# Eight of the 782 row gathers moved from GpSimd's queue to SyncE, and the end of a graph layer's kernel put in another order

## The chip, the cores and the metric

The kernel runs on one core of one Trainium2 chip. The metric is the device time of one execution in microseconds (us). Times are told as the median of several runs; the profile is that of one execution.

## What is computed

There are 6250 nodes with 128 features each and 100,000 edges, which come sorted by their destination. Cut to what matters, the reference is:

```
msg_in = concat([x[src], x[dst], edge_attr])        # 100000 x (128 + 128 + 4)
h = silu(msg_in @ mW1 + mb1)
messages = h @ mW2 + mb2
aggregated = segment_sum(messages, dst)             # 6250 x 128
u = silu(concat([x, aggregated]) @ uW1 + ub1)
updated = u @ uW2 + ub2
y = layer_norm(x + updated) * ln_g + ln_b
out = layer_norm(x + y)
```

## The kernel before, in words

**Tables.** The first layer of the message network is linear before its silu, so the kernel first makes two tables in HBM, one row for each node: `tab_a` holds x @ mW1 for the source's part and `tab_b` x @ mW1 + mb1 for the destination's part (loop over seven parts of x, L367 to L404). The sum of a row of each, and of the attributes' part, is what goes into the silu of an edge.

**Groups of edges.** Edges are taken in 98 groups (`NG`) of 1024, a group being 8 tiles (`G`) of 128 edges; the last group has 6 tiles. For a tile, GpSimd issues one indirect DMA that gathers 128 rows of 512 bytes by the source's index (`fetch`, L273 to L294). The first 5 groups (`RAW`) gather rows of x itself, since the table isn't ready yet; all others gather from `tab_a`. That makes 782 gathers, of which 742 read `tab_a`. Each gather's address list is a column of `src_i`.

**One round of the loop over groups** (L675 to L717), for group g, written out by hand in the order of each engine's queue:

- `load(g + 4)` (L580): SyncE loads 96 rows of `tab_b` from a register address (`mv`, L586) and the attributes of a group (`st`, L587). Every fourth group it loads the destinations of four groups (`near`, L320), and every 14th it reads 14 row numbers into registers (`load_bases`, L344).
- `hidden(g)` (L627): VectorE adds the gathered rows to the product in PSUM, `s = ga + pre` (L635); ScalarE takes the silu into `h` (L636).
- `products(g + 2)` (L614): TensorE makes the destination's and the attributes' part of a later group, `pre` (L618).
- `node_matrix(g + 3)` and `edge_matrix(g + 1)` (L591, L604): VectorE makes 0/1 matrices from the destinations.
- `by_nodes(g)` (L652): TensorE sums `h` by destination into a window of 96 nodes, `pt` (L647); a round or two later `add` puts it into `acc` (L660) and every fourth group the edge counts into `deg` (L665).
- `fetch(g + 2, begun[g + 2], summing[g])` from group 14 on (L703): GpSimd's gathers of two groups ahead. The first of the eight waits for the first matmul of `products(g + 2)`, and the fifth for the first matmul of the sums of group g. The rows have six buffers.

**Nodes.** As soon as all edges of four tiles of nodes are summed, a generator `node_batch` (L466) does the second half of the layer for them. Each `advance` takes it one step on: load xs and copy the sums; three matmuls of y (L509 to L511); silu (L514); one matmul that adds ub2 (L516) and n matmuls with uW2 (L525); the residual and the moments (L527); square root; z and its moments (L534 to L543); square root; shift (L547); the output (L555); its DMA from SyncE (L559). There are 12 such batches of up to 4 tiles; a last one of 2 tiles has to wait for the last edges and is called `final`.

**The end** (L719 to L757). The last group's add, silu and sums are cut into `piece(0, n - 2)` and `piece(n - 2, n)`. In the queue of VectorE the batch next to last (`before`, of 3 tiles) has its step L527 ahead of the first piece and its step L534 to L543 between the two pieces. Then `final` runs its steps from the three matmuls of y on.

Of the kernel before, what the change touches and what calls it, by code (L numbers as in the profile page):

```python
# [8 lines left out]
F32 = mybir.dt.float32  # L9
I32 = mybir.dt.int32  # L10
# [14 lines left out]
def kernel(  # L25
# [57 lines left out]
    MADE = 3  # L83
    NQ = 4
    NM = 5
    BT = 4
    NC = 10
    EC = E // NC
# [177 lines left out]
    ea_d = dram.tile([ED, NG * GE], F32, name="ea_d")  # L266
    near_d = dram.tile([NG, GE], U8, name="near_d")
    rows, bases, near = {}, {}, {}

    def tiles_of(g):  # L270
        return min(G, -(-(E - g * GE) // P))

    def fetch(g, *after):  # L273

        rows[g] = gath.tile([P, G, H], F32, name="ga")
        for i in range(tiles_of(g)):
            ins = nc.gpsimd.indirect_dma_start(  # L277
                out=rows[g][:, i, :],
                out_offset=None,
                in_=x if g < RAW else tab_a[:, :],  # L280
                in_offset=bass.IndirectOffsetOnAxis(
                    ap=src_i[:, g, i : i + 1] if g else src_0[:, i : i + 1], axis=0
                ),
            )
            part, at = divmod(i * len(after), G)
            if after and at == 0 and after[part]:
                tc.add_manual_dep(
                    ins.ins,
                    after[part].ins.name,
                    mybir.DependencyInfo(  # L290
                        mybir.DependencyClass.Sync, mybir.DependencyReason.DATA
                    ),
                    reason="TensorE keeps up with the gathers",
                )  # L294
# [72 lines left out]
    for k, (i0, n) in enumerate(parts):  # L367
        if k + 1 < len(parts):
            turn_x(*parts[k + 1])

        tb = x_sb[:, i0 : i0 + n, :]
        ta = tpool.tile([P, G, H], F32, name="t", bufs=2)
        for j0, m in groups(n, G // 2):
            pm = wide().rearrange("p (i s) f -> p i s f", s=2)
            for j in range(m):
                cols = slice((i0 + j0 + j) * P, (i0 + j0 + j + 1) * P)
                ins = nc.tensor.matmul(pm[:, j], xT[:, cols], w1, start=True, stop=True)  # L377
            own = slice(j0, j0 + m)
            nc.scalar.copy(ta[:, own], pm[:, :m, 0, :])
            nc.vector.tensor_add(  # L380
                tb[:, own], pm[:, :m, 1, :], b1[:, None, :].to_broadcast([P, m, H])
            )
        nc.sync.dma_start(by_node(tab_a)[:, i0 : i0 + n, :], ta[:, :n])
        nc.sync.dma_start(by_node(tab_b)[:, i0 : i0 + n, :], tb)
        table.append(ins)
        if k == 0:
            attributes(0)
        if k == 1:
            fetch(2, *table)
            for t in mv:  # L390
                nc.sync.dma_start(t[W:], mW1[2 * H :])
        if k == 2:
            fetch(3, None, table[2])
        if k == 3:
            destination_lists()
            attribute_rows(0)
            turn_rows(0)
        cols = slice(i0 * P, NW if i0 + n == NT else (i0 + n) * P)
        nc.vector.memset(acc[:, cols], 0.0)
        if k == 4:  # L400
            fetch(4, *table[3:])
            destinations(0)
            load_bases(0)
            turn_rows(1)  # L404
# [27 lines left out]
    ub2_row = consts.tile([1, H], F32, name="ub2_row")  # L432
    g_b = consts.tile([P, H], F32, name="g_b")
    b_b = consts.tile([P, H], F32, name="b_b")
    raw_w = {}

    def load_weights():
        for name, shape in (("w2", [P, H]), ("u1a", [P, H]), ("mb2", [P, 1])):
            raw_w[name] = work.tile(shape, F32, name=f"raw_{name}", bufs=1)
        nc.sync.dma_start(raw_w["w2"], mW2)  # L440
        nc.sync.dma_start(raw_w["u1a"], uW1[P:])
        nc.sync.dma_start(raw_w["mb2"], mb2.rearrange("(f o) -> f o", o=1))
        nc.sync.dma_start(u1x, uW1[:P])
        nc.sync.dma_start(u2, uW2)
        nc.sync.dma_start(ub1_col, ub1.rearrange("(f o) -> f o", o=1))
        nc.sync.dma_start(ub2_row, ub2.rearrange("(o f) -> o f", o=1))
        for t, row in ((g_b, ln_g), (b_b, ln_b)):
            nc.sync.dma_start(t, row.rearrange("(o f) -> o f", o=1).to_broadcast([P, H]))

    def fuse_weights():  # L450
# [15 lines left out]
    def node_batch(i0, n, work, new, y, final=False):  # L466
# [9 lines left out]
        def flat(t):  # L476
            return t[:, :n].rearrange("p i f -> p (i f)")
# [27 lines left out]
        if final:  # L505
            xb = new("xb")
            nc.vector.tensor_add(xb[:, :n], xs[:, :n], b_b[:, None, :].to_broadcast([P, n, H]))
        y = y()
        nc.tensor.matmul(flat(y), u1x, xT[:, cols], start=True, stop=False)  # L509
        nc.tensor.matmul(flat(y), w2u, sums, start=False, stop=False)  # L510
        nc.tensor.matmul(flat(y), mb2u, counts, start=False, stop=True)  # L511
        yield
        uT = new("uT")
        nc.scalar.activation(flat(uT), flat(y), AF.Silu, bias=ub1_col)  # L514
        yield
        nc.tensor.matmul(  # L516
            y[:, :n],
            ones[0:1, :],
            ub2_row[:, None, :].to_broadcast([1, n, H]),
            start=True,  # L520
            stop=False,
        )
        by_p = flat(uT).rearrange("k (p j) -> k p j", j=n)
        for i in range(n):
            nc.tensor.matmul(y[:, i, :], by_p[:, :, i], u2, start=False, stop=i == n - 1)  # L525
        yield
        nc.vector.tensor_add(y[:, :n], y[:, :n], xs[:, :n])  # L527
        mv = moments(y)
# [47 lines left out]
    NST = 5  # L576
    nodes = edges.enter_context(tc.tile_pool(name="nodes", bufs=1))
    stbuf = [held.tile([K1, GE], F32, name=f"st{k}") for k in range(NST)]

    def load(g):  # L580

        if g % NQ == 0 and g:
            destinations(g)
        if g % RB == 0 and g:
            load_bases(g)
        nc.sync.dma_start(mv[g % NM][:W], tab_b[bass.ds(bases[g], W), :])  # L586
        nc.sync.dma_start(stbuf[g % NST][W:], ea_d[:, g * GE : (g + 1) * GE])  # L587
# [39 lines left out]
    def hidden(g):  # L627
        h = hbuf[g % NH]
        ga = rows.pop(g)
        n = tiles_of(g)  # L630
        s = pre.pop(g)
        if g >= RAW:
            ps = s
            s = work.tile([P, G, H], F32, name="s")
            nc.vector.tensor_add(s[:, :n], ga[:, :n], ps[:, :n])  # L635
        nc.scalar.activation(h[:, :n], s[:, :n], AF.Silu)  # L636
        return h

# [36 lines left out]
    for g in range(NG):  # L675
# [10 lines left out]
                attribute_rows(c)  # L686
        if g + LEAD < NG:
            load(g + LEAD)
        last = g >= NG - 1
        if not last:  # L690
            h[g] = hidden(g)
# [21 lines left out]
        for i0, n, first in batches[:-1]:  # L713
            if g == (first if first >= NG - 3 else first + 1):
                running.append(node_batch(i0, n, *node_tiles(nodes, node_y)))
        for _ in range(2 if g >= NG - 6 else 1):
            advance(running)  # L717

    g = NG - 1  # L719
# [18 lines left out]
    )  # L738
    while running:
        advance(running)  # L740
    for _ in range(2):
        next(before)
    next(final)

    nc.scalar.activation(primed, ones[0:1, 0:1], AF.Silu)
    add(g - 1, pt.pop(g - 1))
    pt[g] = degrees(g)
    piece(0, n - 2)
    next(before)
    piece(n - 2, n)  # L750
    add(g, pt.pop(g))
    for _ in range(2):
# [161 lines left out]
```

## Time and profile before

| | |
|---|---|
| median of 3 runs | 1183.07 us (1181.99 to 1183.82) |
| the profiled execution | 1183.82 us, its span 1181.7 us |
| busy share of the span: PE, PEld, DVE, ACT, POOL | 62%, 57%, 41%, 20%, 63% |
| granted TensorE clock, mean | 0.667 |
| gathers from `tab_a` | 742, mean 948 ns of GpSimd each |
| `pre`, `pt` on TensorE | 1564 matmul records each |

The span is the time from the first to the last instruction of the program; the execution's own time has 2.1 us more around it. PE is TensorE's matmul, PEld its loading of weights (it runs beside PE), DVE is VectorE, ACT ScalarE, POOL GpSimd, SPq the queue of SyncE. A group of instructions in the profile is named by its line, engine, operation and "output<-inputs", then its count, its busy time, the mean of one in ns, and the idle time of the engine just before it, with what ended that. "remote" as the one that ended a wait means that the profile can't name it; "issue" is idle time for which the profile shows no wait.

### The profile page before, as it was taken

The page shows a single profiled execution, that of the slowest core. Times are in us where ns is not written, and L with a number is a line of the kernel's source. Part 1 is how long each engine was busy: PE and PEld are TensorE (multiplying, and loading weights), DVE is VectorE, ACT ScalarE, POOL GpSimd, SP SyncE. Part 2 cuts the span into 40 slices and gives each one's busy share as a digit, 9 for nine tenths or more (in the row PEclk, how much of TensorE's full clock was granted, in tenths as well). Part 3 has the DMA queues.
Part 4 walks back from the last instruction along what each step waited for, and adds up shares of the span by engine and source line. Part 5 has one row for each costly group of instructions (what it writes and reads, how often), then busy time and mean ns, then how long its engine had stood idle before and what let it go on. Part 6 is the DMA issues. An engine that isn't in the chain of part 4 may idle for free.

```text
span 1181.7 us, 11311 instructions
## 1 busy us (share of the span) xinstructions
PE 738.3 (62%) x3647; PEld 668.7 (57%) x3647; DVE 486.0 (41%) x1016; ACT 239.8 (20%) x297; POOL 743.1 (63%) x790
## 2 busy tenths in 40 slices
PE   5466887655765566557646655756666665656653
PEld 4465775645655565556645654656565565656552
DVE  4361653432523532532443353343343252353344
ACT  2110120320311221220221121121132131122132
POOL 6546666666666566656666665666566666666660
PEclk9787877666566567566666666666666667666665
DMA  8662232232222231223132222232222222222120
GB/s 200 181 167 73 73 82 64 67 82 64 70 67 73 56 81 50 77 65 84 47 83 71 59 57 80 67 81 56 70 74 66 72 72 62 65 56 69 46 59 20
DMA packets 69932, 88.95 MB, mean 75 GB/s; under 512 B 20687, under 2 KB 51550, under 8 KB 69866
## 3 DMA queue, kind: packets, MB, share of 16 engines
q0 software_dynamic: 25024, 51.30, 17.1%
q1 hardware_dynamic: 40264, 34.96, 10.2%
q10 hardware_dynamic: 4578, 1.89, 0.7%
q8 instruction: 31, 0.51, 0.2%
q14 instruction: 35, 0.29, 0.1%
HBM read 76.71 MB, written 11.38 MB: 75 GB/s over the span
## 4 chain that ended last, share of the span: by engine, by line
PE 44%; issue 35%; POOL 12%; DMA 3%; DVE 2%; another core or an unknown queue 2%; SPq 1%; ACT 1%; DVEq 0%; ACTq 0%; POOLq 0%
PE pre L618 20%; PE pt L647 16%; POOL ga L277 12%; PE y L525 2%; PE wide L377 1%; DMA ga<-tab_a,src_i 1%; PE y L516 1%; PE y L509 1%; PE pre L621 1%; PE y L510 1%; PE wide L339 1%; DVE s L635 1%; DMA x_sb<-in_x_dram 1%; PE y L511 1%
## 5 line engine op out<-in xcount | busy, mean ns | idle before, releaser
L277 POOL DMA_INDIRECT ga<-tab_a,src_i x742 | 703.7, 948 | 383.1 <-issue 200.4
L618 PE MATMUL pre<-mv,st 100*128 100x128 f32 x1564 | 343.3, 393 | 227.3 <-issue 197.6
L618 PEld LDWEIGHTS pre<-mv,st 100*128 100x128 f32 x1564 | 314.2, 300 | 244.5 <-issue 219.3
L647 PE MATMUL pt<-oh,h 128*128 128x96 f32 x1564 | 290.6, 345 | 158.2 <-issue 149.3
L647 PEld LDWEIGHTS pt<-oh,h 128*128 128x128 f32 x1564 | 276.8, 262 | 179.4 <-issue 172.3
L635 DVE TENSOR_TENSOR s<-ga,pre 128x1024 f32<-128x1024 f32 x92 | 112.3, 1221 | 504.1 <-DMA ga<-tab_a,src_i 417.2
L636 ACT ACTIVATE h<-s 128x1024 f32<-128x1024 f32 x92 | 97.2, 1057 | 670.1 <-issue 379.8
L591 DVE TENSOR_SCALAR_CACHE_REDUCE st<-near,p_next 96x1024 f32<-96x1024 uint8 x98 | 124.2, 1268 | 4.2 <-DMA near<-near_d 1.5
L604 DVE TENSOR_TENSOR oh<-w_row,rel 128x768 f32<-128x768 f32 x98 | 93.0, 949 | 39.1 <-remote 36.4
L277 POOL DMA_INDIRECT ga<-in_x_dram,src_i x32 | 30.5, 954 | 21.7 <-issue 8.8
L527 DVE TENSOR_TENSOR y<-y,xs 128x512 f32<-128x512 f32 (+1 forms) x12 | 8.3, 688 | 80.8 <-issue 75.2
L636 ACT ACT_TABLE_LOAD x23 | 29.5, 1283 | 26.4 <-DMA b_b<-in_L_gnn_ln_b_dram 19.5
L489 ACT ACT_TABLE_LOAD x24 | 30.8, 1283 | 6.1 <-DVE st L483 5.7
L525 PEld LDWEIGHTS y<-u,uT 128*128 128x128 f32 x94 | 22.7, 327 | 10.2 <-issue 10.2
L514 ACT ACTIVATE uT<-y,ub_col 128x512 f32<-128x512 f32 (+1 forms) x12 | 8.2, 680 | 98.7 <-remote 58.8
L660 DVE TENSOR_TENSOR acc<-acc,pt 128x96 f32 x98 | 23.6, 241 | 8.9 <-PE pt L647 4.5
L525 PE MATMUL y<-u,uT 128*128 128x128 f32 x94 | 25.2, 416 | 0.0
L665 DVE TENSOR_TENSOR deg<-deg,pt 1x96 f32 x98 | 24.4, 249 | 1.0
L377 PE MATMUL wide<-w,xT 128*128 128x256 f32 x98 | 23.3, 391 | 1.1 <-issue 1.1
L621 PE MATMUL pre<-w,ga 128*128 128x128 f32 x80 | 18.9, 315 | 3.6 <-issue 3.4
L377 PEld LDWEIGHTS wide<-w,xT 128*128 128x128 f32 x98 | 18.8, 198 | 3.9 <-issue 1.5
L555 ACT ACTIVATE z<-z,shift,r 128x128 f32<-128x128 f32 x47 | 19.4, 482 | 0.4 <-DVE shift L549 0.4
(119 smaller groups left out, 357.3 us busy)
## 6 DMA issues: line engine op xcount, KB each, us to landing
ga<-tab_a,src_i POOLq DMA_INDIRECT x742
near<-near_d SPq DMA_DIRECT2D x24, 384.0 KB
mv<-tab_b SPq DMA_DIRECT2D x98, 48.0 KB
tab_a<-t SPq DMA_DIRECT2D x6, 512.0 KB
tab_b<-x_sb SPq DMA_DIRECT2D x6, 512.0 KB
xs<-in_x_dram SPq DMA_DIRECT2D x11, 256.0 KB
out_dram<-z SPq DMA_DIRECT2D x11, 256.0 KB
st<-ea_d SPq DMA_DIRECT2D x98, 16.0 KB
```

Source lines behind the costliest of these rows:

```text
L277: ins = nc.gpsimd.indirect_dma_start(out=rows[g][:, i, :], out_offset=None, in_=x if g < RAW else tab_a[:, :], in_offset=bass.IndirectOffs ...
L377: ins = nc.tensor.matmul(pm[:, j], xT[:, cols], w1, start=True, stop=True)
L489: nc.scalar.activation(r[:, :n], mv[:, :n, 1], AF.Sqrt, bias=eps)
L525: nc.tensor.matmul(y[:, i, :], by_p[:, :, i], u2, start=False, stop=i == n - 1)
L591: nc.vector.tensor_scalar(stbuf[g % NST][:W], near.pop(g), p_next, 0.0, op0=OP.is_equal, op1=OP.add, accum_out=deg_q[g // DQ % 2][:, g % D ...
L604: nc.vector.tensor_tensor(oh, w_row[:, None, :].to_broadcast([P, G, W]), rel[:, g, :, None].to_broadcast([P, G, W]), op=OP.is_equal,)
L618: ins = nc.tensor.matmul(pre[:, i, :], st[:, i, :], mv[g % NM], start=True, stop=g >= RAW)
L621: ins = nc.tensor.matmul(pre[:, i, :], rows[g][:, i, :], w1[:, 0, :], start=False, stop=True)
L635: nc.vector.tensor_add(s[:, :n], ga[:, :n], ps[:, :n])
L636: nc.scalar.activation(h[:, :n], s[:, :n], AF.Silu)
L647: ins = nc.tensor.matmul(pt[:, :W], h[:, i, :], oh[:, i, :], start=i == 0, stop=i == tiles_of(g) - 1)
L665: nc.vector.tensor_add(at, at, pt[row, W:])
```

## The change

It has four parts.

1. **Rows by SyncE.** For the groups 25, 34, 43, 52, 61, 70, 79 and 88 (`by_sync`), `fetch` leaves out the eighth tile. SyncE fetches its 128 rows itself, one DMA of one row (512 bytes) each, spread over nine rounds of the loop, from 11 rounds to 3 rounds ahead of the group: in each round `fetch_by_sync` reads 14 or 15 indices into SyncE's registers and issues as many DMAs. In the first of the nine rounds it loads the 128 indices too. It stands behind `load(g + 4)` in the queue of SyncE. In `hidden`, VectorE's add of such a group is cut in two: the eighth tile from the new buffer first, and then the other seven.
2. **The gathers of group 3**, all of which stood behind the third part of the tables, now stand behind the fourth; the first of them waits for the third part's matmuls and the fifth for the fourth part's.
3. **The final batch** adds ub2 on VectorE to xs, ahead of time, and not with a matmul; its matmul with the counts comes ahead of the one with the sums, and there is a `yield` between the two.
4. **The end.** In the last three rounds `advance` is called four times and not twice. The batch next to last is not stopped ahead of the pieces any more; both pieces follow each other, and the first matmuls of `final` stand ahead of them.

```diff
@@ constants and tables
+    SPAN = 9
...
+    by_sync = {g: None for g in range(CLOSE + SPAN + 2, NG - SPAN + 1, SPAN)}
@@ fetch
-        for i in range(tiles_of(g)):
+        for i in range(tiles_of(g) - (g in by_sync)):
@@ loop over the parts of the tables
-        if k == 2:
-            fetch(3, None, table[2])
         if k == 3:
+            fetch(3, *table[2:])
             destination_lists()
@@ load_weights
+    ub2_b = consts.tile([P, H], F32, name="ub2_b")
...
-        for t, row in ((g_b, ln_g), (b_b, ln_b)):
+        for t, row in ((g_b, ln_g), (b_b, ln_b), (ub2_b, ub2)):
@@ node_batch
             nc.vector.tensor_add(xb[:, :n], xs[:, :n], b_b[:, None, :].to_broadcast([P, n, H]))
+            nc.vector.tensor_add(xs[:, :n], xs[:, :n], ub2_b[:, None, :].to_broadcast([P, n, H]))
         y = y()
         nc.tensor.matmul(flat(y), u1x, xT[:, cols], start=True, stop=False)
-        nc.tensor.matmul(flat(y), w2u, sums, start=False, stop=False)
-        nc.tensor.matmul(flat(y), mb2u, counts, start=False, stop=True)
+        nc.tensor.matmul(flat(y), mb2u, counts, start=False, stop=False)
+        if final:
+
+            yield
+        nc.tensor.matmul(flat(y), w2u, sums, start=False, stop=True)
...
-        nc.tensor.matmul(
-            y[:, :n],
-            ones[0:1, :],
-            ub2_row[:, None, :].to_broadcast([1, n, H]),
-            start=True,
-            stop=False,
-        )
+        if not final:
+            nc.tensor.matmul(
+                y[:, :n],
+                ones[0:1, :],
+                ub2_row[:, None, :].to_broadcast([1, n, H]),
+                start=True,
+                stop=False,
+            )
         by_p = flat(uT).rearrange("k (p j) -> k p j", j=n)
         for i in range(n):
-            nc.tensor.matmul(y[:, i, :], by_p[:, :, i], u2, start=False, stop=i == n - 1)
+            nc.tensor.matmul(y[:, i, :], by_p[:, :, i], u2, start=final, stop=final or i == n - 1)
@@ new
+    def fetch_by_sync(g):
+
+        for to in by_sync:
+            k = g - (to - SPAN - 2)
+            if not 0 <= k < SPAN:
+                continue
+            lo, hi = k * P // SPAN, (k + 1) * P // SPAN
+            if k == 0:
+                by_sync[to] = work.tile([P, H], F32, name="ga_s")
+                sources = work.tile([1, P], I32, name="src_s")
+                e0 = (to * G + G - 1) * P
+                nc.sync.dma_start(sources, src[e0 : e0 + P].rearrange("(o p) -> o p", o=1))
+                source_rows[to] = sources
+            _, vals = nc.values_load_multi_w_load_instructions(
+                source_rows[to][0:1, lo:hi],
+                engines=(ENG.SP,),
+                min_val=0,
+                max_val=N - 1,
+                skip_runtime_bounds_check_because=IN_RANGE,
+            )
+            for p, v in zip(range(lo, hi), vals):
+                nc.sync.dma_start(by_sync[to][p : p + 1, :], tab_a[bass.ds(v, 1), :])
@@ hidden
+            if g in by_sync:
+                n -= 1
+                nc.vector.tensor_add(s[:, n], by_sync[g], ps[:, n])
             nc.vector.tensor_add(s[:, :n], ga[:, :n], ps[:, :n])
+            n = tiles_of(g)
@@ loop over the groups
             load(g + LEAD)
+        fetch_by_sync(g)
...
-        for _ in range(2 if g >= NG - 6 else 1):
+        for _ in range(4 if g >= NG - 3 else 2 if g >= NG - 6 else 1):
             advance(running)
@@ the end
-    for _ in range(2):
-        next(before)
     next(final)
...
     pt[g] = degrees(g)
+    next(final)
     piece(0, n - 2)
-    next(before)
     piece(n - 2, n)
     add(g, pt.pop(g))
     for _ in range(2):
```

More of the change, by code (lines that the diff above doesn't have):

```diff
@@ L578 @@
     stbuf = [held.tile([K1, GE], F32, name=f"st{k}") for k in range(NST)]
+    def fetch_by_sync(g):
[19 more added lines that the diff above has]
+                nc.sync.dma_start(by_sync[to][p : p + 1, :], tab_a[bass.ds(v, 1), :])
+    source_rows = {}
     def load(g):
```

## The prediction

> **What bounds the kernel now.** I read first the page's costliest groups. The gathers take 703.7 us of GpSimd, 948 ns each, and VectorE's add of the gathered rows stands idle for 417.2 us until a gather has landed:
>
> ```profile
> L277 POOL DMA_INDIRECT ga<-tab_a,src_i x742 | 703.7, 948 | 383.1 <-issue 200.4
> L635 DVE TENSOR_TENSOR s<-ga,pre 128x1024 f32<-128x1024 f32 x92 | 112.3, 1221 | 504.1 <-DMA ga<-tab_a,src_i 417.2
> ```
>
> Next the table by windows; in each row a busy time and a count for each engine, then clock, DMA share and GB/s. The first is the steady part of the loop, the second one short stretch in it:
>
> ```profile
> 181.00:1109.00 928.00, 576.25 (x2758) 527.27 (x2757) 369.18 (x772) 182.16 (x217) 606.84 (x640) 0.64 0.25 68
> ...
> 592.60:598.30 5.70, 0.93 (x6) 0.53 (x5) 3.66 (x13) 0.06 (x1) 2.05 (x3) 0.76 0.25 56
> ```
>
> In the steady part there are 640 gathers in 928 us, 1.45 us each. The timeline of GpSimd shows what that is made of:
>
> ```profile
> 593.06 0.95 POOL L277 DMA_INDIRECT ga<-tab_a,src_i  x1 [0.31 <-issue]
> 594.31 0.95 POOL L277 DMA_INDIRECT ga<-tab_a,src_i  x1 [0.30 <-issue]
> 598.62 0.94 POOL L277 DMA_INDIRECT ga<-tab_a,src_i  x1 [3.36 <-remote]
> 599.87 0.94 POOL L277 DMA_INDIRECT ga<-tab_a,src_i  x1 [0.30 <-issue]
> ```
>
> A gather starts every 1.25 us (0.95 and 0.30), and ahead of every 16th stands a pause of 3.4 us. 16 x 1.25 and 3.2 more are 23.2 us for two groups, 11.6 us a round, as the window has it. The waits say what the pauses are put down to:
>
> ```profile
> DVE s L635 <- DMA ga<-tab_a,src_i: 417.2, 63, 10.2
> POOL ga L277 <- remote: 141.1, 47, 3.6
> POOL ga L277 <- PE pre L618: 18.1, 13, 3.5
> ```
>
> Only 18.1 us, and two rows of 8.8 and 7.1, are put down to matmuls that a gather waits for. So from 181 to 1151 us GpSimd's queue is the bound. In the second window TensorE nearly stands still too (0.93 us busy of 5.7), just ahead of the pause's end. What makes the pause I can't tell; that it comes once in 16 gathers I can.
>
> **What the Trainium skill says.** "DMA: Bandwidth & Descriptors", section SWDGE vs HWDGE vs iDMA: GpSimd builds its DMAs' descriptors in software, SyncE's are made by hardware. The trace agrees: 0.95 us of GpSimd for a gather, about 0.33 us of SyncE for an issue. The same page, section Issuing engines are not separate DMA queues: another issuing engine saves only the issue time, since all share the DMA engines. Here these are 0.25 busy in the steady part, so issue time is what is at stake. Its section Latency and other measured facts gives a floor of about 600 ns for a tensor_load into registers; the trace has 620 ns at least, but 3087 in the median:
>
> ```profile
> L344 SPq TENSOR_LOAD <-base_i x7: 620/3087/3363, 63.6 to 930.7; - x7
> ```
>
> **Part 1, what it removes.** Eight gathers of 1.25 us: 10.0 us of the queue that is the bound. Half a pause less (8/16 x 3.4): 1.7 us, of which I take 1.6; the bounds are 0 and 1.7. What is late next is TensorE, for which the first and fifth gather of a group wait. Around 590 us it begins `pre` of group 50 at 588.3 and the sums of group 48 at 591.6, while the gathers that wait for them start at 598.6 and 603.6: 10 us of room, and 1.25 us in nine groups doesn't use it up. But the pause now falls one gather later for each removed one, in the middle of groups, and TensorE's standstill moves with it; in a few rounds a gather already waits for TensorE (the 13 above). From 0 to 10 us; I take +2.
>
> **Part 1, what it adds.** On VectorE one add of 128x128 (0.24 us is the row of `acc`, 128x96) and a shorter main add: it is done before the other seven tiles land, so nothing; without that cover 8 x 0.25 = 2 us. On the DMA engines 1024 rows, 0.5 MB of 89 MB: nothing. On SyncE, in 72 rounds, one read of 14 or 15 registers and as many DMAs. Two stretches of SyncE's timeline price them, one near the loop's start, one after a wait late in the loop:
>
> ```profile
> 73.91 0.33 SPq L586 DMA_DIRECT2D mv<-tab_b  x1
> 74.28 0.33 SPq L587 DMA_DIRECT2D st<-ea_d  x1
> 74.79 0.33 SPq L586 DMA_DIRECT2D mv<-tab_b  x1
> ...
> 82.01 0.25 SPq L446 DMA_DIRECT2D ub_row<-in_L_gnn_ub_dram  x1
> ```
>
> ```profile
> 926.50 1.41 SPq L586 DMA_DIRECT2D mv<-tab_b  x1
> 927.94 0.33 SPq L587 DMA_DIRECT2D st<-ea_d  x1
> 929.25 0.00 SPq L586 DMA_DIRECT2D mv<-tab_b  x1
> 929.27 0.24 SPq L587 DMA_DIRECT2D st<-ea_d  x1
> ```
>
> In the first, a DMA with a register address takes 0.51 us from start to start (0.88 for the pair less 0.37), of which 0.33 is the issue; a row of 512 bytes was issued in 0.25 us, so 0.43 for a row. In the second, four DMAs take over 3 us, 0.8 each. No trace of before has a long run of single rows: from 0.43 to 0.9 us. I take 0.45, since in most of the round nothing slows the queue. The read: 0.6 to 3.4 us, I take 2.3, the mean of the seven. SyncE's own work: 0.88 for `mv` and `st`, and about 0.35 a round for destinations, registers, xs, attributes and outputs. Sum: 14.2 x 0.45 + 2.3 + 1.2 = 9.9 us of a round of 11.6. So it is hidden, with 1.7 us to spare. What is queued behind it is the next `load` and the outputs: a load is wanted two rounds later, so SyncE may fall some 23 us behind before TensorE waits for `mv` and `st`. What it costs without the cover is the first rival.
>
> **Part 2.** Group 4's first gather starts at 49.4 us, its fifth at 60.6 (it waits for the fifth part of the tables), group 5's first at 73.5 (it waits for the table's landing). With group 3 behind the fourth part, its last four end near 54.5 and group 4's first four near 59.5, still before 60.6: nothing. Bounds -1 and +2.
>
> **Parts 3 and 4.** The end in the timeline, with the batch's residual, the two pieces, and the matmul of ub2:
>
> ```profile
> 1155.67 0.57 DVE L527 TENSOR_TENSOR y<-y,xs 128x384 f32<-128x384 f32 x1 [5.56 <-PE y L525]
> ...
> 1159.13 0.69 DVE L727 TENSOR_TENSOR s<-ga,pre 128x512 f32<-128x512 f32 x1
> ...
> 1163.22 0.40 DVE L727 TENSOR_TENSOR s<-ga,pre 128x256 f32<-128x256 f32 x1
> ...
> 1168.47 1.22 PE L516 MATMUL pre<-ub_row,ones 1*128 1x256 f32 x2 [0.57 <-ACT ga L514]
> ```
>
> From the second piece on all is one chain to the end. Out of it go the counts' matmul (0.85 us from start to start) and L516 (1.1 us): 2.0 us. The second piece follows the first at once and not 3.4 us later. Against that, VectorE's two adds of `final` (0.4 us each) now stand ahead of the pieces, and they wait for the DMA of xs, issued at 1158.4; a landing of 2.6 us, as the gathers have it, would put the pieces behind 1161. So of 3.4 us I count 2.5. The batch's steps ahead of the pieces use VectorE's 5.6 us of idle time before 1155.67, since its matmuls no longer stand behind the sums of group 96. Together -4.5; bounds -7 and +2, the latter if TensorE's queue waits for the batch's silu in front of those sums.
>
> **The sum.** -10.0 - 1.6 + 2 + 0 - 4.5 = -14.1 us. The profiled execution took 1183.8 us (span 1181.7 and 2.1 around it), which gives 1169.7; it lies 0.75 above the median of the runs, so I say 1169.0, in a range of 1162 to 1177.
>
> **Rivals.**
> (a) *SyncE becomes the bound.* For it: after every wait its queue shows spells like that at 926 us, and TensorE's standstills take SyncE with them. It decides from a row of 0.57 us on: (11.6 - 3.5) / 14.2. At 0.63 us a round is 12.45, 0.85 over; in 72 rounds 61 us, less the 23 of lead, less the 4.5 of the end: 1217. At 0.9 it would be several hundred. Against it: 0.43 near the loop's start.
> (b) *TensorE takes back the gain.* The moved pauses meet rounds with a node batch and gathers wait for TensorE, 10 us and not 2; 1177, and up to 1180.
> (c) *SyncE's lateness eats just what the rest wins*, or the parts don't do what they say: 1183.
>
> **Chances.** Forecast 0.48, (b) 0.12, (c) 0.07, (a) 0.33. A measurement of this kernel can tell about 0.2% (2.4 us) from no change: faster 0.60, same 0.07, slower 0.33. The range reaches from 1162, with 0.05 below it, to 1225, which leaves the worse part of (a), 0.15, above it.
>
> **What would show it.** Right: 742 gathers become 734 at 1.25 us, with a pause still at each 16th; VectorE's add still waits for gathers; SyncE has idle time in each round, rows 0.45 us apart. Wrong: TensorE's `pre` or VectorE's `st` waiting for DMA `mv`, `st` or `near`; rows over 0.57 us apart; idle time in front of L635 that ends with a row of SyncE. At the end, the pieces within 1 us of each other and no L516 behind the last silu.

## The result, and the profile after

The changed kernel takes **1384.67 us** (median of 6 runs, 1376.37 to 1387.04), the kernel before 1183.62 us (6 runs, 1181.99 to 1185.12): a ratio of 1.169, 95% interval 1.166 to 1.172. The forecast was 1169. What came is rival (a), SyncE as the bound, and worse than it was priced.

The kernel before, measured beside each experiment on its chip, took 1014 to 1017 us beside thirteen of them and 1174 to 1181 us beside five (one chip showed both), so a number is compared only within its level. I call these **the 1016 level and the 1180 level**; the result belongs to the second. The mean granted TensorE clock of the kernel before was 0.72 to 0.75 on the first and 0.66 to 0.68 on the second, but a gather took some 0.94 us of GpSimd on both, so it isn't slower gathers that make the second level.

The groups of the changed kernel that answer to the two of before, and a third:

```profile
L279 POOL DMA_INDIRECT ga<-tab_a,src_i x734 | 692.5, 944 | 602.2 <-issue 200.0
L670 DVE TENSOR_TENSOR s<-ga,pre 128x1024 f32<-128x1024 f32 (+1 forms) x92 | 111.0, 1207 | 292.6 <-DMA ga<-tab_a,src_i 223.6
L623 DVE TENSOR_SCALAR_CACHE_REDUCE st<-near,p_next 96x1024 f32<-96x1024 uint8 x98 | 124.4, 1270 | 394.5 <-DMA near<-near_d 391.5
```

A gather still costs GpSimd 0.944 us, but GpSimd now idles 602 us ahead of its gathers and not 383. VectorE waits less for gathers (224 us against 417), and its `st` stands idle for 394.5 us (4.2 before), 391.5 of them for `near`, a DMA of SyncE's. The table by windows, in the rounds with rows:

```profile
400.00:800.00 400.00, 189.17 (x945) 172.08 (x945) 132.52 (x285) 65.39 (x76) 203.01 (x216) 0.63 0.18 53
```

216 gathers in 400 us are 1.85 us each, where the kernel before had 1.45. The waits, first of the consumers and of GpSimd, then those of SyncE's own queue:

```profile
DVE st L623 <- DMA near<-near_d: 391.5, 18, 32.5
PE pre L650 <- DMA st<-ea_d: 202.9, 24, 14.6
POOL ga L279 <- PE pt L683: 157.4, 23, 11.9
POOL ga L279 <- PE pre L650: 129.3, 35, 9.6
POOL ga L279 <- remote: 101.1, 40, 3.7
```

```profile
SPq L497 <- DVE st L485: 38.3, 1, 38.3
SPq L566 <- ACT z L562: 26.1, 2, 15.9
```

This is the picture of a late queue: VectorE and TensorE wait for SyncE's loads, GpSimd waits for TensorE, and SyncE itself waits little for others (its longest entry is 38.3 us in total; before it was 186.8). Its timeline shows at what (start, length, DMAs in a row; the rows are L608):

```profile
590.01 0.30 SPq L618 DMA_DIRECT2D mv<-tab_b  x1
...
593.67 16.45 SPq L608 DMA_DIRECT2D ga_s<-tab_a  x14
610.37 0.32 SPq L618 DMA_DIRECT2D mv<-tab_b  x1
610.75 0.31 SPq L619 DMA_DIRECT2D st<-ea_d  x1
614.41 10.11 SPq L608 DMA_DIRECT2D ga_s<-tab_a  x14
625.25 0.00 SPq L497 DMA_DIRECT2D xs<-in_x_dram  x1
625.44 0.32 SPq L618 DMA_DIRECT2D mv<-tab_b  x1
```

Two rounds, from `mv` to `mv` 20.4 and 15.1 us; the same 14 rows take 16.45 us in one and 10.11 in the other. And one level lower, by source line (shortest, median, longest in ns), first the rows, then the register read:

```profile
L608 SPq FUSED_REGOPS  x1024: 1/37/1397, 173.7 to 1257.3; - x171
L608 SPq MOVE ga_s<-tab_a x1024: 2/29/1396, 173.8 to 1257.7; - x171
L608 SPq DMA_DIRECT2D ga_s<-tab_a x1024: 2/228/1353, 173.9 to 1257.7; - x171
```

```profile
L600 SPq TENSOR_LOAD <-src_s x72: 143/2584/3346, 172.3 to 1243.5; - x72
```

A row is three instructions. In the median they take 37, 29 and 228 ns, and a row follows the last after 0.42 us. But there are spells in which each of the three takes 0.70 us, or 1.40, so that a row takes 2.1 us or more. I count as a spell a stretch of 1.3 us or more in which SyncE's instructions, register reads apart, start 0.6 to 0.8 or 1.3 to 1.5 us after one another; such stretches cover 456 us of the run. Summing SyncE's queue from start to start over the 72 rounds gives 1084 us: 760 for rows (0.742 each), 180 for reads (with the gap ahead of each), 144 for the rest. **That is 10.56 + 2.50 + 2.00 = 15.05 us a round**, against the 11.6 of GpSimd.

### The profile page after: what moved, and what is told of

Read it like the earlier page. It is cut to its first block, busy times and chain, and to the rows that moved or that the text cites. A ratio compares the mean times of both kernels' runs of the same rounds, so it can differ in the third digit from the quotient of the medians.

```text
span 1385.2 us, 14499 instructions
## 1 busy us (share of the span) xinstructions
PE 726.7 (52%) x3645; PEld 650.7 (47%) x3645; DVE 487.5 (35%) x1025; ACT 239.3 (17%) x297; POOL 731.9 (53%) x782
## 5 line engine op out<-in xcount | busy, mean ns | idle before, releaser
L279 POOL DMA_INDIRECT ga<-tab_a,src_i x734 | 692.5, 944 | 602.2 <-issue 200.0
L650 PE MATMUL pre<-mv,st 100*128 100x128 f32 x1564 | 321.0, 379 | 341.8 <-DMA st<-ea_d 202.9
L650 PEld LDWEIGHTS pre<-mv,st 100*128 100x128 f32 x1564 | 296.7, 286 | 364.7 <-issue 346.7
L683 PE MATMUL pt<-oh,h 128*128 128x96 f32 x1564 | 283.4, 347 | 263.3 <-DVE acc L696 179.8
L683 PEld LDWEIGHTS pt<-oh,h 128*128 128x128 f32 x1564 | 269.7, 262 | 275.0 <-issue 232.9
L623 DVE TENSOR_SCALAR_CACHE_REDUCE st<-near,p_next 96x1024 f32<-96x1024 uint8 x98 | 124.4, 1270 | 394.5 <-DMA near<-near_d 391.5
L670 DVE TENSOR_TENSOR s<-ga,pre 128x1024 f32<-128x1024 f32 (+1 forms) x92 | 111.0, 1207 | 292.6 <-DMA ga<-tab_a,src_i 223.6
L313 ACT COPY ea_t<-ea_l 80x500 f32<-80x500 f32 x10 | 10.8, 1080 | 181.6 <-DMA ea_l<-in_edge_attr_dram 181.4
L279 POOL DMA_INDIRECT ga<-in_x_dram,src_i x32 | 30.3, 948 | 17.4 <-issue 8.5
L523 PE MATMUL y<-ub_row,ones 1*128 1x512 f32 (+1 forms) x24 | 23.5, 1078 | 8.5 <-ACT uT L520 8.5
```

Source lines behind the costliest of these rows:

```text
L279: ins = nc.gpsimd.indirect_dma_start(out=rows[g][:, i, :], out_offset=None, in_=x if g < RAW else tab_a[:, :], in_offset=bass.IndirectOffs ...
L623: nc.vector.tensor_scalar(stbuf[g % NST][:W], near.pop(g), p_next, 0.0, op0=OP.is_equal, op1=OP.add, accum_out=deg_q[g // DQ % 2][:, g % D ...
L650: ins = nc.tensor.matmul(pre[:, i, :], st[:, i, :], mv[g % NM], start=True, stop=g >= RAW)
L683: ins = nc.tensor.matmul(pt[:, :W], h[:, i, :], oh[:, i, :], start=i == 0, stop=i == tiles_of(g) - 1)
```

## The experiments

Of each edit the lines that matter are shown. The theory after the result: the loop takes the length of SyncE's queue, and the spells make that long. Rivals: parts 2 to 4 have a share; the 1024 small DMAs themselves do the harm; the register reads do; or that run was slow for a reason that has nothing to do with the queue.

### Which part of the change, and what the eight gathers are worth

```diff
e1_without_rows (and e15):
+    by_sync = {}
e2_rows_only: the kernel before, with by_sync, fetch_by_sync and the cut add alone
e3_seven_tiles:
-        fetch_by_sync(g)
-                nc.vector.tensor_add(s[:, n], by_sync[g], ps[:, n])
+                nc.vector.tensor_add(s[:, n], ga[:, 0], ps[:, n])
e4_fixed_rows (and e12, e16): no register read, and
+                v = (to * 131 + p * 37) % N
+                nc.sync.dma_start(by_sync[to][p : p + 1, :], tab_a[v : v + 1, :])
```

> The whole change but for its first part: GpSimd gathers all tiles of all groups, and SyncE fetches no row. Theory (SyncE's row fetching is the whole loss): 1178 to 1184 us, that is the kernel before less what the other order of the end gives, of which the prediction held 4.5 us and the profile after shows only 0.3. Rival (a part of the loss lies in parts 2 to 4, for example at the start or the end): above 1190 us.

> The kernel before with the first part of the change alone. Theory: SyncE's queue is the bound in the 72 rounds, so 1384 to 1390 us, the changed kernel to within 5 us. Rival (the parts together make the loss): clearly under 1370 us.

> The changed kernel without fetch_by_sync: nobody fetches the eighth tile of the eight groups; VectorE's separate add takes the first tile's rows a second time. That part of the computation is left out. It gives what the eight gathers taken from GpSimd are worth if the rows cost nothing. Theory (prediction's sum for the removal, 11.6 less 2 for TensorE): 9 to 12 us below the run without rows, about 1168 to 1172 us. Rival (the pause of 3.4 us or TensorE eats the removal): within 4 us of the run without rows.

> The changed kernel with rows at fixed addresses: SyncE issues the same 1024 DMAs of one row of 512 bytes in the same places, but each is one instruction in place of three, and nothing is read into registers. The rows are other rows of the table, so this part of the computation is changed. Theory (SyncE's instructions cost it the time, each 0.70 us in the slow spells): a round needs 14.2 x 0.25 to 0.4 and 1.8 of its own, 6 to 8 us of 11.6, so SyncE is hidden again: 1168 to 1180 us. Rival (1024 small DMAs, their packets or the DMAs in flight are what slows the loop): stays above 1300 us.

All four fell on the 1016 level (kernel before 1016.37 us).

| run | median us | ratio, 95% interval |
|---|---|---|
| e1, without rows | 1012.70 | 0.9969 (0.9961 to 0.9978) |
| e2, rows only | 1018.82 | 1.0034 (1.0017 to 1.0051) |
| e3, eighth tile by nobody | 1003.33 | 0.9888 (0.9866 to 0.9909) |
| e4, rows at fixed addresses | 1003.74 | 0.9884 (0.9859 to 0.9909) |

The numbers expected for all four were those of the 1180 level. Measured from the kernel before, e1, e3 and e4 came out on the side of the theory; e2, expected at 1384, missed by far. The trace of e1 says why: its list of GpSimd's waits has no "remote" any more. The pauses of 3.4 us, 141 us in the trace of the kernel before, are gone, and 592 gathers in a row follow each other 1.25 us apart (the kernel before itself has no trace on this level):

```profile
POOL ga L279 <- issue: 219.2, 719, 0.3
POOL ga L279 <- DMA ga<-tab_a,src_i: 9.4, 31, 0.3
POOL ga L279 <- DMA tab_a<-t: 4.8, 1, 4.8
```

SyncE has no spells on this level either: in e2 the rows stand 0.41 us apart in the median and 0.42 in the mean. Still the rows aren't free. The eight gathers taken off GpSimd are worth 1012.70 - 1003.33 = 9.4 us, and 1024 small DMAs at fixed addresses in their place cost nothing measurable (e4), but the rows as the change fetches them win nothing.

### The change again, and what in SyncE's round is long

```diff
e5_after_again: the changed kernel
e6_one_read: the read only in the first of the 72 rounds, its 15 registers used in all
e7_span_18:
-    SPAN = 9
+    SPAN = 18
e8_reads_only: the reads stay, no row is issued
-                nc.sync.dma_start(by_sync[to][p : p + 1, :], tab_a[bass.ds(v, 1), :])
```

> The changed kernel itself, once more. In the four runs before, the kernel of before took 1016.4 us and not 1183, its gathers followed each other without the pauses of 3.4 us, and SyncE's rows stood 0.41 us apart in the median and 0.43 in the mean. Theory (SyncE is the bound; how much it costs hangs on the spells in which each of its instructions takes 0.70 us, and these come and go with the pauses): beside a kernel before of some 1016 us the changed kernel takes 1012 to 1018 us (1018.8 for the rows alone, 3.7 less for the rest); beside one of some 1183 us it takes 1376 to 1390. Rival (the row fetching costs 17% everywhere and the rows-only run was slow for less because it lacked the other parts): 15 to 18% over the kernel before in either case.

> The changed kernel with 15 indices read into SyncE's registers once, in the first of the 72 rounds, and used in all of them: the rows are issued as before, three instructions each, but 71 of 72 register reads are gone. Other rows of the table are fetched, so this part of the computation is changed. Theory: a round of SyncE is shorter by the read (2.6 us measured without spells, 2.4 with them). Without spells 10.6 less 2.6 is 8 us, under the gathers' 10.0, so hidden: 1002 to 1006 us beside 1016. With spells 15.05 less 2.4 is 12.65 in 72 rounds, 170 us less than the change: 1205 to 1225 beside 1183. Rival (the read stalls the queue by waiting for the rows in flight, so it is the whole loss): at the kernel before or under it in both cases.

> The changed kernel with SPAN = 18: three groups (34, 52, 70) instead of eight, each spread over 18 rounds, so 7 or 8 rows a round in 54 rounds. Theory: with spells SyncE needs 7.1 x 0.74, 2 for the read and 2 of its own, 9.3 us of 11.6, so it is hidden: the run without rows (1179 to 1183) less 3 x 1.45, 1174 to 1180. Without spells 7.1 x 0.43 and 4 is 7 of 10.0: 1012.7 less 3.75, 1008 to 1011. Rival (rows disturb the loop by something that is not the length of SyncE's queue, in proportion to their number): with spells 3/8 of 200 us lost, some 1255.

> The changed kernel with the register reads kept and the rows not issued: nobody fetches the eighth tile of the eight groups, and VectorE's separate add takes the first tile's rows a second time; that part of the computation is left out. Theory (the rows' instructions make the length of the queue): a round of SyncE is 2.4 to 2.6 for the read and 2 of its own, so it is hidden, and the run gains the eight gathers: 1002 to 1005 us beside 1016, or 1165 to 1173 beside 1183. Rival (the read is what stalls): as slow as the change.

Again the 1016 level (kernel before 1016.42 us).

| run | median us | ratio, 95% interval |
|---|---|---|
| e5, the changed kernel | 1016.63 | 1.0002 (0.9991 to 1.0014) |
| e6, one read | 1003.61 | 0.9871 (0.9845 to 0.9896) |
| e7, SPAN 18 | 1010.90 | 0.9941 (0.9919 to 0.9963) |
| e8, reads only | 1004.27 | 0.9870 (0.9844 to 0.9896) |

All four came as the theory had them. Here the changed kernel is **as fast as the kernel before**, which shows the loss of 17% to hang on the level. A round of SyncE in e5 (761.5 us for 72) is 6.01 for rows, 2.79 for the read and 1.78 for the rest, 10.58 us; GpSimd's is 8 x 1.25 = 10.0. So SyncE is the bound even without a spell, by a little, and it costs 1016.63 - 1003.61 = 13.0 us, which eats the whole gain. It is less than the queue itself lost: from the first read to the last row the traces have 763 us in e5 and 716 in e6, so some 34 of these 47 us seem to go into the lead that SyncE has over the others (an estimate from these figures). Taking away the read or the rows puts it under 10 us and brings the gain back. A calm round of the changed kernel, to lay beside those above:

```profile
593.70 5.62 SPq L608 DMA_DIRECT2D ga_s<-tab_a  x14
599.57 0.32 SPq L618 DMA_DIRECT2D mv<-tab_b  x1
599.95 0.31 SPq L619 DMA_DIRECT2D st<-ea_d  x1
603.61 5.61 SPq L608 DMA_DIRECT2D ga_s<-tab_a  x14
```

The same 14 rows take 5.62 us where they took 16.45 and 10.11. The gap of some 3.5 us between `st` and the next rows is the read.

### A dose, and ways out

```diff
e9_three_reads: ahead of each read, two more of the same indices into other registers
e10_half_by_act: half of each round's indices and rows in ScalarE's queue, behind the silu
+        fetch_by_sync(g, nc.scalar, ENG.Activation, 1)
e11_span_11:
-    SPAN = 9
+    SPAN = 11
```

> The changed kernel with two further register reads of the same 14 or 15 indices ahead of the one whose values are used, so that SyncE's work of a round grows by some 5.3 us and nothing else of the change moves. In the changed kernel beside a kernel before of 1016 us, 72 rounds of SyncE's queue took 761.5 us, 10.6 each; two reads of 2.64 make 15.9, near to the 15.05 that the traced run of the change had beside 1183. Theory (the loop takes the length of SyncE's queue): 1016.6 + 72 x 5.28 = 1397 us, 1385 to 1405, beside 1016 us; beside a kernel before of 1183 (a read there is 2.37) 1384 + 72 x 4.7 = 1725. Rival (the result's 200 us came from whatever made that run slow everywhere, and the length of SyncE's queue has little to do with it): under 1250 us beside 1016.

> The changed kernel with every round's rows in two halves: 7 or 8 by SyncE, and as many by ScalarE's queue, which reads its own indices and issues them behind the silu of the round. ScalarE stands idle for over half of each round. Theory: SyncE's round falls to 7.1 x 0.43 + 2 + 2 = 7 us (9.7 with the row of 0.74), under the gathers', so the eight gathers are won: 1002 to 1006 us beside 1016, 1164 to 1174 beside 1183, and this beats both kernels. Rival (ScalarE's queue becomes late, 5 us of rows and read between two silus, and the node batches' steps with it): 1008 us or more beside 1016.

> The changed kernel with SPAN = 11: six groups (27, 38, 49, 60, 71, 82), 11 or 12 rows a round in 66 rounds. Theory: a round of SyncE is 11.6 x 0.43 + 2.4 + 1.9 = 9.3 us, under the gathers' 9.98, so it is hidden: 1012.7 less 6 x 1.25 = 1005 us, 1003 to 1007 beside 1016. Beside 1183 the row of 0.74 makes it 8.6 + 2.2 + 2 = 12.8, over 11.6 by 1.2 in 66 rounds, 79 us less some 40 of lead: about 1210. Rival (SyncE delays the loop already below its full load, since a load that comes late in a round is late for its user): 1010 us or more.

These three fell on the 1180 level (kernel before 1174.01 us).

| run | median us | ratio, 95% interval | SyncE's round, us | a row, us |
|---|---|---|---|---|
| e9 | 1380.75 | 1.177 (1.172 to 1.183) | 14.9 | 0.73 |
| e10 | 1197.61 | 1.018 (1.015 to 1.021) | 12.4 | 1.19 |
| e11 | 1279.31 | 1.091 (1.089 to 1.092) | 13.7 | 0.82 |

e9 was no dose: its trace has 72 reads for rows and not 216, so the reads whose values nobody uses didn't run. It is the changed kernel once more, and so shows that the result comes again at the same level.

e10 and e11 both missed, on the slow side. The direction is right, fewer instructions of SyncE and a shorter round; but the price of a row is no constant. The fewer rows SyncE has, **the more each row costs**, 0.73, 0.82 and 1.19 us. Spells cover 422 us in e11 and 514 in e10. One reason, argued from the traces alone, is that SyncE holds GpSimd up less: of the time of the rows' rounds, 0.43 in e9, 0.51 in e11 and 0.56 in e10 lies more than 3 us into a run of gathers that nothing interrupts, and there most of the spells lie (see below). Of e10's 1.19 us 0.07 is another thing: rows that wait for earlier rows to land (34.6 us in all). ScalarE has such waits too, and all that stands behind them in its queue waits with them:

```profile
ACT L491 <- DMA ga_s<-tab_a: 68.7, 8, 25.7
ACT z L562 <- DMA ga_s<-tab_a: 63.0, 8, 18.2
```

### The dose again, and half the gathers

```diff
e14_reads_in_thirds: in each round three reads of 5 indices, each followed by its 5 rows
+            for a in range(lo, hi, 5):
+                b = min(a + 5, hi)
e13_half_the_gathers (and e17, e18):
+        for i in range(min(G // 2, tiles_of(g)) if g >= CLOSE else tiles_of(g)):
```

> Once more the changed kernel with rows at fixed addresses: 1024 DMAs of one row each, one instruction a row in place of three, nothing read into registers (other rows are fetched, so this part of the computation is changed). Theory (each instruction of SyncE takes 0.70 us in the spells, and their number makes the queue long): beside a kernel before of some 1180 us, a third of the rows' 0.74 us a row and no read, 3.5 to 6 us for rows and 2 of its own in a round of 11.4: hidden, or nearly, 1158 to 1185. Rival (the 1024 small DMAs themselves bring on the spells): above 1300. Beside a kernel before of 1016 us again 1002 to 1006.

> The changed kernel with four gathers for a group instead of eight from group 14 on; VectorE's add takes each of the four tiles' rows twice, so that part of the computation is left out. SyncE's rows stay as they are. Beside a kernel before of some 1180 us the spells of SyncE lie mostly in trains of gathers 1.25 us apart, and end when GpSimd stands still. Theory A (the gathers bring on the spells): SyncE's rows come 0.43 to 0.5 us apart, its round is 10.6 to 11.5, and the loop takes that or TensorE's own time: 1000 to 1120 us. Theory B (the spells come with SyncE's own row DMAs): rows stay 0.7 us apart and the time above 1300. Beside a kernel before of 1016 us SyncE's round of 10.6 us stays the bound and the time stays 1005 to 1020.

> The changed kernel with each round's read split in three, each of 5 values and followed by the rows of its values; rows, addresses and results are those of the change. Theory (a read that follows DMAs costs 2.4 to 2.8 us, whatever its length, and the loop takes the length of SyncE's queue): 5.2 us more in 72 rounds: 1016.6 + 375 = 1392 us, 1370 to 1405, beside a kernel before of 1016; 1384 + 340 = 1725 beside one of 1183. Rival A (the read costs by its values, 0.19 us each): as the change, 1016 to 1020 or 1375 to 1390. Rival B (the queue's length isn't what the loop takes): less than half of the addition although the trace shows the longer queue.

> Once more all but the first part of the change: no row fetched by SyncE, all gathers by GpSimd. Theory: 3 to 5 us under the kernel before in either case (3.7 measured beside 1016; the forecast had 4.5): 1178 to 1181 beside 1183, 1169 to 1171 beside 1174. Rival (the other order of the end costs where instructions are slow, as the profile after with its 30.3 us from the last gather to the end against 30.6 suggests): no gain, within 1 us of the kernel before.

The 1016 level once more (kernel before 1016.64 us): e12 1004.15 us (ratio 0.9883, 0.9856 to 0.9910), e13 966.90 (0.952, 0.950 to 0.955), e14 1077.66 (1.060, 1.057 to 1.064), e15 1012.97 (0.9964, 0.9951 to 0.9977). e12 and e15 repeat e4 and e1. e13 came 38 us under its expectation on this level: SyncE's 72 rounds still took 738.7 us there, 10.3 each, but in the other rounds there were now half the gathers to wait for.

e14 lies between its theory (1370 to 1405) and its rival A (1016 to 1020) and is yet the cleanest proof. The reads didn't cost 2.6 us each; the source lines of e5, e7 and e14 show that they cost mostly by their values (14 or 15, 7 or 8, up to 5), with some 0.3 us for each read on top (an estimate from the medians of e5 and e7):

```profile
L600 SPq TENSOR_LOAD <-src_s x72: 1331/3118/3344, 139.1 to 892.6; - x72
```

```profile
L600 SPq TENSOR_LOAD <-src_s x54: 782/1714/1828, 136.5 to 665.3; - x54
```

```profile
L602 SPq TENSOR_LOAD <-src_s x216: 563/1312/1488, 137.8 to 958.6; - x108
```

So the dose was 0.86 us a round and not 5.2. SyncE's 72 rounds grew from 761.5 us (e5) to 823.7, by 62.2 us, and **the kernel by 1077.66 - 1016.63 = 61.0 us**: what is added to SyncE's queue comes out at the end, one for one.

### The cause on the 1180 level

> Once more the changed kernel with rows at fixed addresses: 1024 DMAs of one row each, one instruction a row in place of three, nothing read into registers (other rows are fetched, so this part of the computation is changed). Theory (each instruction of SyncE takes up to 0.70 us in the spells, and reads and register instructions are two thirds of the queue): beside a kernel before of some 1180 us hidden or nearly, 1158 to 1185. Rival (the 1024 small DMAs themselves bring on the spells and make the queue long): above 1300. Beside a kernel before of 1016 us again 1002 to 1006.

e16 fell on the 1180 level: **1176.72 us beside 1180.66** (0.9951, 0.9931 to 0.9970). As many DMAs of one row, to fixed addresses, with a third of the instructions and without the reads, and the 200 us are gone; the small DMAs are not the cause. There are still spells, some 359 us of them, with single instructions of up to 1.46 us:

```profile
L602 SPq DMA_DIRECT2D ga_s<-tab_a x1024: 2/250/1455, 172.0 to 998.7; - x171
```

But a row is one instruction now and took 0.456 us in the mean, against 0.742. SyncE's round was 11.48 us, now with waits in it. The gain is smaller than on the other level, though, 3.9 us and not 12.6. GpSimd's pauses are where to look for the rest; they come to 22 us more than the 141.1 us of the kernel before, on 60 places and not 47:

```profile
POOL ga L279 <- remote: 163.4, 60, 3.7
POOL ga L279 <- PE pre L644: 12.0, 7, 3.5
```

From the first gather of `tab_a` to the last, GpSimd takes 1076.3 us in e16 and 1077.7 in the kernel before, although eight gathers, 10 us, are missing; of the 6.5 us between the spans of these two traces 5.0 lie ahead of that, in a first gather that starts earlier (part 2).

What brings on the spells? In the trace of the changed kernel, from the first of SyncE's rows to the last, I sorted time by how long GpSimd had been issuing gathers without a break (1.25 us apart; I call that a train). In the first 3 us of a train 0.07 of the time lies in a spell, from 3 to 8 us 0.57, from 8 to 14 us 0.89; later than 3 us after the start of a train's last gather, 0.04.

GpSimd's pause seems to be the same thing seen from another queue. From group 14 on the kernel before has 45 breaks of over 1 us between gathers and e16 has 59, and all of them stand ahead of the first or the fifth gather of a group, the two for which the kernel has GpSimd wait. Between such places a train runs on through a spell, and at the next one GpSimd stops, in most cases for some 2.1, 2.8 or 3.5 us, three to five times 0.70. No run tests this.

> The changed kernel with four gathers for a group instead of eight from group 14 on; VectorE's add takes each of the four tiles' rows twice, so that part of the computation is left out. SyncE's rows stay as they are. Beside a kernel before of some 1180 us: theory A (trains of gathers bring on the spells): SyncE's rows come 0.43 to 0.5 us apart in the mean, its round takes 10.3 to 11.5 us, spells take up under 60 us of the run and the time is 1000 to 1110 us. Theory B (the spells come with SyncE's own instructions and DMAs): rows 0.65 to 0.75 us apart, spells over 300 us, time above 1300. Beside a kernel before of 1016 us again 965 to 969.

> As the run before it: four gathers for a group instead of eight from group 14 on, each of the four tiles' rows used twice; SyncE's rows as in the change. Beside a kernel before of some 1180 us: theory A (trains of gathers bring on the spells): rows 0.43 to 0.5 us apart in the mean, spells under 60 us of the run, 1000 to 1110 us. Theory B (the spells come with SyncE's own instructions and DMAs): rows 0.65 to 0.75 us apart, spells over 300 us, above 1300. Beside a kernel before of 1016 us again 965 to 969.

e17 fell on the 1016 level: 966.28 us beside 1014.04 (0.9535, 0.9519 to 0.9551), as e13. e18 fell on the 1180 level: **1103.45 us** (four runs, 1096.39 to 1113.80) **beside 1174.82** (0.939, 0.932 to 0.946). Half of the gathers from group 14 on are left out there, so its time is no gain; what counts is SyncE's queue, which is that of the change. Two of its rounds:

```profile
591.09 7.25 SPq L608 DMA_DIRECT2D ga_s<-tab_a  x14
598.44 0.37 SPq L497 DMA_DIRECT2D xs<-in_x_dram  x1
...
603.11 6.48 SPq L608 DMA_DIRECT2D ga_s<-tab_a  x14
```

Of the 100 trains 84 are of four gathers now, spells cover 104 us and not 456, a row takes 0.515 us and SyncE's round 11.57. That is theory A, with a rest of spells (104 us where it had expected under 60, and a row just above its 0.5). So GpSimd's gathers bring on most of the slow spells of SyncE on that level. That it is the length of a train, and not the number of gathers in all, rests on the sorting above, since e18 halved both; and a train alone isn't enough, since the 592 gathers in a row of e1 on the other level brought on none. What it is in the chip that a train uses up, and why the level changes, stays open; no run here shows it.

## Why the prediction was wrong

**The failed step** is the sum for SyncE, "9.9 us of a round of 11.6. So it is hidden, with 1.7 us to spare", and in it the row of 0.45 us, taken "since in most of the round nothing slows the queue". Term by term:

| us a round | predicted | measured, 1180 level | 1016 level (e5) |
|---|---|---|---|
| 14.2 rows | 6.4 | 10.56 | 6.01 |
| register read | 2.3 | 2.50 | 2.79 |
| SyncE's own work | 1.2 | 2.00 | 1.78 |
| sum | 9.9 | 15.05 | 10.58 |
| GpSimd's round before | 11.6 | 11.6 | 10.0 |

The fast row was right (0.42 in e5). What failed is that a mean was needed and the row of the calm was taken. The views shown with the prediction would have given part of that: stretches like that of 5.7 us in which TensorE nearly stood still come once in some 23.2 us of that trace, and the four DMAs at 926 us, at 0.8 each, showed what SyncE does in one. A quarter of the time at 0.8 us a row and the rest at 0.43 is 0.52 in the mean and a round of 10.9 us, 0.7 to spare and not 1.7 (an estimate from these figures). What those views do not show is that the spell holds each instruction, and a row has three: 2.1 us. With that, in a round of 11.6 us, 2.85 us of spell give 1.4 rows, and the other 8.75, less the 3.5 of read and own work, give 12.2 rows at 0.43: 13.6, and 14.2 were needed. Nothing was to spare even so; and in the changed kernel spells took up 427 of the 1084 us of the rows' rounds, 0.39 and not a quarter.

**Rival (a)** named the mechanism, the point from which it decides (0.57 us a row) and the signs: `pre` waiting for `st`, VectorE's `st` waiting for `near`. With the measured row its own formula gives 14.2 x 0.742 + 3.5 = 14.0, 175 us over 72 rounds, 1331 us; the other two terms, 1.0 us a round too small (72 us in all), more than cover the 54 that are left. It had 0.33 of the chance, and its range was cut at 1225 although "several hundred" stood in its text: the upper bound of the row, 0.9, was not carried into the range.

**The bound before** was read rightly: e3 takes eight gathers of 1.25 us away and wins 9.4 us of the 10.0 on the 1016 level, where no pause is in the way; the +2 for TensorE isn't seen there. On the 1180 level the -1.6 for half a pause had the wrong sign. e16, with SyncE's queue shortened, wins 3.9 us where -14.1 was forecast for a hidden SyncE, and its pauses grew by 22 us. The pause was held to come "once in 16 gathers" and to fall one gather later for each removed one; it doesn't go by the count. All of them stand where a gather has to wait for TensorE, and with eight gathers gone they still fall at the start of every second group at the end of the loop (groups 88, 90, 92 and 94).

**VectorE's add and the DMA engines**, nothing: right on the 1016 level (e4 is within 0.4 us of e3).

**Part 2**, nothing, bounds -1 and +2: not so in the trace on the 1180 level. The first gather from `tab_a`, at 73.47 us before, started at 69.10. I had followed GpSimd's queue alone; the pause ahead of group 4 and the tables' DMAs moved forward with it:

```profile
56.39 0.94 POOL L279 DMA_INDIRECT ga<-in_x_dram,src_i  x1 [2.79 <-PE wide L363]
...
69.10 0.94 POOL L279 DMA_INDIRECT ga<-tab_a,src_i  x1 [8.03 <-DMA tab_a<-t]
```

**Parts 3 and 4**, -4.5: parts 2 to 4 together give 3.7 us, twice, on the 1016 level, so the size was about right there. On the 1180 level they weren't run alone; in the trace of the change the end gives almost nothing, 30.3 us from the last gather's start to the end of the span against 30.6. The two pieces do follow each other, but as feared behind the wait for xs, 12.0 us after the last gather, where the first had been 8.0 after it:

```profile
1365.96 0.42 DVE L509 TENSOR_TENSOR ga<-ga,b_b 128x256 f32<-128x256 f32 x1 [1.42 <-DMA ga<-in_x_dram]
1366.42 0.42 DVE L510 TENSOR_TENSOR ga<-ga,ub_b 128x256 f32<-128x256 f32 x1
1366.88 1.02 DVE L764 TENSOR_TENSOR s<-ga,pre 128x512 f32<-128x512 f32 x2
```

**The register read** was priced by the mean of seven reads, near the truth. The Trainium skill has the better rule, which I had not used: "Runtime: NRT & Kernel Launch", section Instruction fetch mechanics, puts a read into registers at about 200 ns a register, in bulk too. The traces agree but for the 0.3 us on top: 3118 ns in the median for 14 or 15 values, 1714 for 7 or 8, 1312 for up to 5.

**What is better?** With all rows in place, SPAN 18 beats both kernels on the 1016 level (1010.90 us, 0.9941). It wasn't run on the 1180 level, where none of the versions with the true rows was under the kernel before; parts 2 to 4 alone give 0.3% on the 1016 level and were not run on the other.

## What to carry to other kernels

Work moved to an idle queue is hidden only if the whole queue fits in the shortest round: count its instructions, not its DMAs (a row at a register's address was three, and its index 0.2 us more), and price them with the share of time in which the trace shows that queue crawling, not with the median. Where the price of the added work has an upper bound that makes a new engine the bound, that case belongs in the range up to its end. And a queue that others wait for (here `mv`, `st`, `near`) is a bad place for work that nobody is in a hurry for.

## What was not expected of the hardware

- The kernel before has two levels, 1016 and 1180 us, also on one and the same chip. On the first, gathers run without pauses (e1) and SyncE's instructions without spells (e2, e5); on the second GpSimd pauses for up to 3.6 us after a long train of gathers, at the next gather that has to wait for TensorE, and SyncE's instructions take 0.70 us each for 0.57 of the time from 3 to 8 us into a train and 0.89 from 8 to 14 us.
- A register-addressed DMA of one row costs SyncE 0.42 us in the calm and 2.1 us or more in a spell; one with a fixed address, a single instruction, 0.32 us (e12) and 0.456 us in the mean on the 1180 level (e16).
- Fewer rows made each row dearer (0.73, 0.82, 1.19 us), while more of the time lay in long trains of gathers (0.43, 0.51, 0.56 of it beyond a train's first 3 us).
